# Graph attention with batch and layer norm on one core: 21 rows a group on the Sync queue in place of 16, and turned places stored so that four groups are one run

## The chip, the cores and the metric

The kernel runs on one core of a Trainium2 chip. The metric is the device time of one execution in microseconds (us), taken as the median of several runs. The core's engines are PE (matrix products), DVE (vector), ACT (activations), POOL (GpSimd, which issues the indirect gathers) and SP (Sync, which issues ordinary DMAs). Each engine runs its own instructions in order; between engines they wait on semaphores.

## The reference

There are N = 12500 nodes of 128 features and E = 212500 edges, sorted by destination. Cut to what matters:

```python
Q, K, V = x @ WQ, x @ WK, x @ WV               # 8 heads of 16
Eh = edge_attr @ WE
score = exp(clip((K[src] * Q[dst] / 4 * Eh).sum(-1), -5, 5))   # per head
wV = segment_sum(V[src] * score, dst); Z = segment_sum(score, dst)
h = x + wV / (Z + 1e-6)
h = batchnorm(h) * gamma + beta                # over the nodes
out = layernorm(x + h)                         # over the features
```

## The kernel before, in words

The edges are 1661 tiles of 128. A window is 4 tiles whose destinations lie within 64 nodes; a group is two windows, 8 tiles, and there are 208 groups. First a table `kvd` of K and V rows (1 KB a node) is written to DRAM. Then the main loop (L793 to L840) takes one group an iteration, with the stages of neighbouring groups interleaved by hand: the order in which the code is written is the order on each engine.

**Where K and V rows come from.** POOL gathers one tile, 128 rows of 1 KB, with one indirect DMA (L230). It does this for 8 tiles of a group, into one of 9 slots; a slot comes free after the group's last use (`message`, L615). In some groups, those that `row_plan` (L58) names, the 8th tile is not gathered by POOL. SP fetches it row by row (`fetch_rows`, L273): it loads 16 byte offsets into registers with one instruction (L275) and issues 16 DMAs of 1 KB (L282), in every iteration from 8 on. 128 rows take 8 iterations, so that there are 24 such groups, and the last rows are fetched in iteration 199. `products` and `message` treat the 8th tile of such a group with an instruction of its own (`parts`, L270).

**What else SP does.** In iteration g, in this order: `load(g + 4)` (L492), 512 KB of edge features into one of three `ea` buffers, which must wait until PE has used group g + 1; `load_rel`, for the few groups without a quad; in every fourth iteration `load_quad` (L389), which brings the places of four groups, turned, to all partitions as two DMAs of 256 KB (`rbq`), one for each half of the partitions, four runs of 1 KB for a partition; then `fetch_rows(g)`. From iteration 199 on, `load_x` (L476) loads pieces of the transposed x into slots that have come free. PE needs the `ea` of group g + 2 in iteration g (`ehqe`, L560).

**Places.** `place(r)` (L375) computes the place of each edge's destination in its window for 64 windows at a time, turns the columns of 128 tiles with PE, and writes them through ACT's queue into `relT` in DRAM (L385). The first run is done during the table stage, the others at the end of iterations 20, 52, 84, 116, 148, 180 and 195 (two short ones).

Of the kernel before, what the change touches and what calls it, by code (L numbers as in the profile page):

```python
# [8 lines left out]
F32 = mybir.dt.float32  # L9
BF16 = mybir.dt.bfloat16  # L10
# [7 lines left out]
P = 128  # L18
# [3 lines left out]
G = 8  # L22
U = 4
WN = 64
# [5 lines left out]
ROWS = P  # L30
FIRST_ROW = 8
ROW_LAG = 3
ROW_STREAMS = (("SP", 16),)
RQ = 4


# [3 lines left out]
def plan(N, T):  # L40

    n, r = divmod(T - sum(LAST), U)
    sizes = [U] * n + [r] * (r > 0) + list(LAST)
    assert n > 1 and len(sizes) % 2 == 0
    starts = [sum(sizes[:g]) for g in range(len(sizes))]
    cuts = list(range(0, N - 64, CH)) + [N - 64, N]
    due = {}
    thr = [0.0] * len(sizes)
    for j, c in enumerate(cuts[1:]):
        need = (c + (64 if c < N - CH else 24)) * T  # L50
        g = next((g for g, t in enumerate(starts) if t * N >= need), None)
        if g is not None:
            due.setdefault(g, []).append(j)
            thr[g] = float(c)
    return sizes, starts, cuts, due, thr


def row_plan(sizes):  # L58


    full = sizes.count(U) // 2
    used, plan_ = set(), []
    for _, n in ROW_STREAMS:
        groups, end = [], 0
        while True:
            end += P
            g = FIRST_ROW + -(-end // n) - 1 + ROW_LAG
            while g in used:
                g += 1
            if g >= full:  # L70
                break
            used.add(g)
            groups.append(g)
        plan_.append(groups)
    return plan_
# [7 lines left out]
def gnn_kernel(  # L83
# [19 lines left out]
    nc = tc.nc  # L103
    N, D = out.shape
    T = src.shape[1]
    NW = dstb.shape[1]
    usizes, ustarts, cuts, due, _ = plan(N, T)
# [8 lines left out]
    dram = ctx.enter_context(tc.tile_pool(name="dram", bufs=1, space=bass.MemoryType.DRAM))  # L116
# [4 lines left out]
    wp = lps.enter_context(tc.tile_pool(name="work", bufs=2))  # L121
# [2 lines left out]
    late = []  # L124

    kvd = dram.tile([N, 2 * P], F32, name="kvd")
    relT = dram.tile([T, P], BF16, name="relT")

# [30 lines left out]
    rel = rel_i.bitcast(F32)  # L161
# [28 lines left out]
    ident = consts.tile([P, P], F32, name="ident")  # L190
# [24 lines left out]
    def slot(i):  # L215
        return rows.tile([P, 2 * G * P], F32, name=f"slot{i}")
# [35 lines left out]
    cols = ids = 0  # L252
    for (_, n), groups in zip(ROW_STREAMS, row_plan(usizes)):
        tot = len(groups) * P
        for q in range(-(-tot // n)):
            at = (q % P, cols + q // P * n, min(n, tot - q * n))
# [3 lines left out]
        if tot % n:  # L260
            q = tot // n
# [33 lines left out]
    for g in range(nxg):  # L295
        if g % 2 == 0:
            PAIR[g // 2] = free.pop(0)
            t = slot(PAIR[g // 2])
# [52 lines left out]
    def vw(a, r):  # L351
        return a[:, ustarts[r[0]]:ustarts[r[0]] + (r[1] - r[0]) * r[2]].rearrange("p (g k) -> p g k", k=r[2])

    def bc(a, r):
        return a[:, r[0]:r[1], None].to_broadcast([P, r[1] - r[0], r[2]])
# [19 lines left out]
    def place(r):  # L375
        nc.vector.tensor_copy(vw(rel, r), vw(rel_i, r))
        nc.vector.tensor_tensor(vw(rel, r), vw(rel, r), bc(base_f, r), op=OP.subtract)
        end = ustarts[r[0]] + (r[1] - r[0]) * r[2]
        for t in range(ustarts[r[0]], end, P):
            n = min(P, end - t)  # L380
            ps = spare_ps
            nc.tensor.transpose(ps[:n], rel[:, t:t + n], ident)
            row = wp.tile([P, P], BF16, name="relrow", bufs=2)
            nc.vector.tensor_copy(row[:n], ps[:n])
            nc.scalar.dma_start(relT[t:t + n, :], row[:n])  # L385

    RB = {}

    def load_quad(q):  # L389
        t = late[0].tile([P, RQ, U * P], BF16, name="rbq", bufs=2)  # L390
        for h in (0, 1):
            at = ustarts[2 * RQ * q + h] * P
            nc.sync.dma_start(t[h * WN:(h + 1) * WN], bass.AP(
                tensor=relT.tensor, offset=relT.offset + at, ap=[[0, WN], [G * P, RQ], [1, U * P]]))
        for k in range(RQ):
            RB[RQ * q + k] = t[:, k, :]

# [2 lines left out]
    def load_rel(g):  # L400
        if g // RQ in quads:
            return
        RB[g] = wp.tile([P, U * P], BF16, name="rb", bufs=3)
        for h in (0, 1):
            t, n = ustarts[2 * g + h], usizes[2 * g + h]
            nc.sync.dma_start(RB[g][h * WN:(h + 1) * WN, :n * P],
                              bass.AP(tensor=relT.tensor, offset=relT.offset + t * P, ap=[[0, WN], [1, n * P]]))

    mv = consts.tile([P, 2], F32, name="mv")
    ab = consts.tile([P, 2], F32, name="ab")  # L410
# [290 lines left out]
    def both_halves(g):  # L701
        both(g, 0)
        both(g, 1)


    steps = [[(locate,)], [(place, runs[0])], [], [(q_mm, 0), (q_hi, 0)],
             [(q_mid, 0), (load_rel, 0)], [(q_lo, 0), (load, 0)], [(q_mm, 1), (q_hi, 1), (load_rel, 1)],
             [(q_mid, 1)], [(q_lo, 1), (load_rel, 2)], [(load, 1)], [(turned_onehot, 0)],
             [(turned_onehot, 1)]]
    first_step = NQ - len(steps) - 5  # L710
    assert first_step > 3 and max(piece) < first_step + 14
    windows = {first_step + 2: (0, 1), first_step + 8: (2,)}
    for q in range(NQ):
# [13 lines left out]
        k = q - first_step  # L727
# [16 lines left out]
    within(load, 2)  # L744
    turned_onehot(2)
    load_rel(3)
    q_window(3)
    load_rel(4)
# [44 lines left out]
    for g in range(NG - 2):  # L793
        within(load, g + 4)
        within(load_rel, g + 5)
        if (g + 6) % RQ == 0 and (g + 6) // RQ in quads:
            load_quad((g + 6) // RQ)
# [30 lines left out]
        for r in runs[1:]:  # L828
            if g == max(4, r[0] // 2 - 12):
                place(r)  # L830
# [16 lines left out]
    g = last - 1  # L847
# [326 lines left out]
```

## Time and profile before

| what | value |
|---|---|
| median of 3 runs (lowest to highest) | 2110.27 us (2109.47 to 2112.22) |
| the profiled execution's own time | 2108.13 us |
| its span (first to last instruction) | 2106.3 us |
| mean granted PE clock | 0.925 |
| busy PE, DVE, POOL, ACT | 1692.8, 1633.1, 1579.5, 635.8 us |
| gathers from `kvd` by POOL | 1573, of 948 ns |
| row DMAs by SP | 3072, of 1 KB |
| `ea`, `rbq` DMAs by SP | 208 of 512 KB (one smaller), 94 of 256 KB |
| DMA moved | 386.83 MB, 184 GB/s on average |

Times in views count from the start of the span. "Idle before, releaser" says how long an engine stood still ahead of an instruction and what ended that. SP does no counted work, so its load is read from its timeline: a row there gives the start, the length and the number of DMAs that were merged into it. Register loads are not in it, so the hole of about 1.35 us between an `ea` and the first row is mostly the load of the 16 offsets.

### The profile page before, as it was taken

The page shows a single profiled execution, that of the slowest core. Times are in us where ns is not written, and L with a number is a line of the kernel's source. Part 1 is how long each engine was busy: PE and PEld are TensorE (multiplying, and loading weights), DVE is VectorE, ACT ScalarE, POOL GpSimd, SP SyncE. Part 2 cuts the span into 40 slices and gives each one's busy share as a digit, 9 for nine tenths or more (in the row PEclk, how much of TensorE's full clock was granted, in tenths as well). Part 3 has the DMA queues.
Part 4 walks back from the last instruction along what each step waited for, and adds up shares of the span by engine and source line. Part 5 has one row for each costly group of instructions (what it writes and reads, how often), then busy time and mean ns, then how long its engine had stood idle before and what let it go on. Part 6 is the DMA issues. An engine that isn't in the chain of part 4 may idle for free.

```text
span 2106.3 us, 37679 instructions
## 1 busy us (share of the span) xinstructions
PE 1692.8 (80%) x9414; PEld 1106.6 (53%) x9414; DVE 1633.1 (78%) x3601; ACT 635.8 (30%) x2480; POOL 1579.5 (75%) x1673
## 2 busy tenths in 40 slices
PE   8899888888777787777778778777777777787777
PEld 6665555555455455445455555554454544454457
DVE  3559989988777778787778787778777778777787
ACT  2353333333222222222222223222222223223225
POOL 7777777777777777777777777777777777777775
PEclk9999989999999999899998898899999999899999
DMA  8956656666566555566565566665566565565684
GB/s 284 306 183 187 188 174 192 188 188 190 166 188 187 175 169 166 159 187 187 177 176 159 165 182 187 178 177 158 168 188 177 177 176 158 166 187 149 181 269 129
DMA packets 177913, 386.83 MB, mean 184 GB/s; under 512 B 38862, under 2 KB 94711, under 8 KB 177687
## 3 DMA queue, kind: packets, MB, share of 16 engines
q0 software_dynamic: 77552, 210.48, 34.1%
q1 hardware_dynamic: 95972, 171.08, 26.7%
q10 hardware_dynamic: 4163, 2.79, 0.4%
q8 instruction: 77, 1.26, 0.2%
q14 instruction: 149, 1.22, 0.2%
HBM read 364.58 MB, written 19.63 MB: 182 GB/s over the span
## 4 chain that ended last, share of the span: by engine, by line
DVE 23%; POOL 22%; DMA 21%; issue 16%; PE 13%; SPq 2%; ACT 2%; DVEq 1%; ACTq 0%; POOLq 0%
POOL slot L230 22%; DMA slot<-kvd,srcs 15%; DVE wt L578 6%; DVE msg L621 4%; DVE s L603 3%; DMA rbq<-relT 3%; PE ps_a L636 3%; PE ps_e L565 2%; DVE p L597 2%; DVE oh L526 2%; DMA ea<-eaT 2%; SPq L282 1%; PE ps_t L586 1%; DVE ot L536 1%; PE ps_m L661 1%
## 5 line engine op out<-in xcount | busy, mean ns | idle before, releaser
L230 POOL DMA_INDIRECT slot<-kvd,srcs x1573 | 1491.0, 948 | 480.5 <-issue 415.2
L636 PE MATMUL ps_a<-msg,oh 128*128 128x136 f32 (+1 forms) x3322 | 555.9, 309 | 0.5 <-DVE msg L621 0.5
L597 DVE TENSOR_TENSOR p<-slot,ps_t 128x512 f32<-128x512 f32 (+1 forms) x410 | 269.2, 672 | 309.8 <-DMA slot<-kvd,srcs 254.2
L636 PEld LDWEIGHTS ps_a<-msg,oh 128*128 128x128 f32 (+1 forms) x3322 | 450.0, 178 | 84.1 <-issue 60.7
L565 PE MATMUL ps_e<-ea,w_e 128*128 128x512 f32 x832 | 438.1, 653 | 32.3 <-DMA ea<-eaT 30.7
L612 ACT ACTIVATE ps_m<-s 128x64 f32<-128x64 f32 (+1 forms) x209 | 47.5, 227 | 1226.0 <-DVE s L611 920.2
L586 PE MATMUL ps_t<-ident,wt 128*128 128x128 f32 x1661 | 249.5, 293 | 113.1 <-DVE wt L578 111.4
L578 DVE TENSOR_TENSOR wt<-wt,ps_q 128x512 f32<-128x512 f32 x416 | 265.6, 680 | 13.0 <-PE ps_q L573 12.5
L661 PE MATMUL ps_m<-ident,at 128*128 128x128 f32 x412 | 99.0, 324 | 218.3 <-DVE oh L529 214.5
L586 PEld LDWEIGHTS ps_t<-ident,wt 128*128 128x128 f32 x1661 | 197.1, 148 | 141.9 <-DVE wt L578 135.3
L567 ACT ACTIVATE wt<-ps_e 128x512 f32<-128x512 f32 x416 | 233.9, 586 | 71.8 <-PE ps_e L565 67.7
L603 DVE TENSOR_REDUCE s<-p 128x64 f32<-128x1024 f32 (+1 forms) x209 | 251.9, 1205 | 0.1
L621 DVE TENSOR_TENSOR msg<-slot,ps_m 128x1024 f32<-128x1024 f32 (+2 forms) x209 | 244.7, 1173 | 1.0 <-ACT ps_m L612 0.7
L565 PEld LDWEIGHTS ps_e<-ea,w_e 128*128 128x128 f32 x832 | 158.3, 212 | 154.4 <-issue 115.8
L661 PEld LDWEIGHTS ps_m<-ident,at 128*128 128x128 f32 x412 | 64.5, 197 | 310.1 <-ACT q L555 283.8
L573 PE MATMUL ps_q<-ot,q 64*128 64x512 bf16 x1248 | 173.1, 384 | 0.0
L573 PEld LDWEIGHTS <-q 64*128 64x128 bf16 x1248 | 44.3, 95 | 195.7 <-issue 171.8
L526 DVE TENSOR_TENSOR oh<-ps_m,rel_i 128x512 f32<-128x512 f32 x208 | 142.0, 683 | 0.0
L515 ACT ACTIVATE xw<-hx 128x64 f32 x416 | 83.9, 248 | 65.2 <-issue 53.0
L652 DVE SCALAR_TENSOR_TENSOR at<-os,keep,rz 128x128 f32<-128x128 f32 x208 | 73.2, 352 | 26.2 <-PE ps_m L661 1.5
L666 ACT ACTIVATE hx<-ps_m 128x64 f32 x412 | 90.4, 219 | 7.9 <-PE ps_m L662 1.2
L546 PE MATMUL ps_m<-w_q,xw 128*128 128x128 f32 x416 | 85.9, 290 | 3.2 <-DVE oh L529 2.8
(173 smaller groups left out, 1549.5 us busy)
## 6 DMA issues: line engine op xcount, KB each, us to landing
ea<-eaT SPq DMA_DIRECT2D x207, 512.0 KB
byrow<-kvd SPq DMA_DIRECT2D x3072, 1.0 KB
slot<-kvd,srcs POOLq DMA_INDIRECT x1573
rbq<-relT SPq DMA_DIRECT2D x94, 256.0 KB
kvd<-slot SPq DMA_DIRECT2D x12, 512.0 KB
kvd<-t SPq DMA_DIRECT2D x12, 512.0 KB
slot<-xT SPq DMA_DIRECT2D x24, 256.0 KB
out<-o SPq DMA_DIRECT2D x23, 256.0 KB
```

The costliest lines, as they stand in the source:

```text
L230: return nc.gpsimd.indirect_dma_start(out=out, out_offset=None, in_=table, in_offset=bass.IndirectOffsetOnAxis(ap=srcs[:, e:e + 1], axis=0))
L526: nc.vector.tensor_tensor(one, iota_ps[:, None, :].to_broadcast([P, n, P]), r[:, :n, None].to_broadcast([P, n, P]), op=OP.is_equal)
L565: nc.tensor.matmul(eh, w_e, EA[g][:, a:b, :].rearrange("p a b -> p (a b)"), start=True, stop=True)
L567: nc.scalar.activation(t[:, :(b - a) * P], eh, AF.Copy)
L573: nc.tensor.matmul(QE[g][h], Q3[g][r, k, :], OT[g][r, :(b - a) * P], start=(k == 0), stop=(k == 2))
L578: nc.vector.tensor_tensor(t, t, QE[g][h], op=OP.mult)
L586: nc.tensor.transpose(ps[:, j, :], WT[g][h][:, j * P:(j + 1) * P], ident)
L597: nc.vector.tensor_tensor(PR[g][:, c:d, :], KV[g](c, d, 0), PW[g][i][:, c - a:d - a, :], op=OP.mult)
L603: nc.vector.tensor_reduce(SS[g][:, a:b, :], PR[g][:, a:b, :].rearrange("p t (h d) -> p t h d", d=DH), axis=AX.X, op=OP.add)
L621: nc.vector.tensor_tensor(MSG[g][:, a:b, :P].rearrange("p t (h d) -> p t h d", d=DH), KV[g](a, b, P).rearrange("p t (h d) -> p t h d", d=D ...
L636: nc.tensor.matmul(AGG[g][WN if j >= n else 0:], OH[g][j], MSG[g][:, j, :], start=(j == 0), stop=(j == n - 1))
L661: nc.tensor.matmul(ps, AT[g], ident, start=True, stop=False)
```

## The change

SP fetches 21 rows an iteration in place of 16. By `row_plan`, 32 groups in place of 24 get their 8th tile this way, in iterations 8 to 203 (the last has one row); POOL has 8 gathers fewer. The turned places are kept as two DRAM tensors, one for the even windows (first half of the partitions) and one for the odd, so that four groups' places for a half are one contiguous run, and a partition gets one run of 4 KB in place of four of 1 KB. For that `place` first collects the columns of the even and then those of the odd windows in a staging tile (two DVE copies), turns that, and writes two DMAs in place of one. The number of turns is the same.

```diff
-ROW_STREAMS = (("SP", 16),)
+ROW_STREAMS = (("SP", 21),)
...
-    relT = dram.tile([T, P], BF16, name="relT")
+    at_half, half_rows = [], [0, 0]
+    for w, k in enumerate(usizes):
+        at_half.append(half_rows[w % 2])
+        half_rows[w % 2] += k
+    relT = [dram.tile([n, P], BF16, name=f"relT{h}") for h, n in enumerate(half_rows)]
...
     def place(r):
         nc.vector.tensor_copy(vw(rel, r), vw(rel_i, r))
         nc.vector.tensor_tensor(vw(rel, r), vw(rel, r), bc(base_f, r), op=OP.subtract)
-        end = ustarts[r[0]] + (r[1] - r[0]) * r[2]
-        for t in range(ustarts[r[0]], end, P):
-            n = min(P, end - t)
+        k = r[2]
+        for w in range(r[0], r[1], P // (2 * k) * 2):
+            z = min(w + P // (2 * k) * 2, r[1])
+            stage = wp.tile([P, 4, P], F32, name="xt", bufs=2)[:, 0, :]
+            spans, n = [], 0
+            for v in range(w, min(w + 2, z)):
+                c = len(range(v, z, 2))
+                nc.vector.tensor_copy(stage[:, n:n + c * k].rearrange("p (g k) -> p g k", k=k),
+                                      vw(rel, r)[:, v - r[0]:z - r[0]:2, :])
+                spans.append((v, n, c * k))
+                n += c * k
             ps = spare_ps
-            nc.tensor.transpose(ps[:n], rel[:, t:t + n], ident)
+            nc.tensor.transpose(ps[:n], stage[:, :n], ident)
             row = wp.tile([P, P], BF16, name="relrow", bufs=2)
             nc.vector.tensor_copy(row[:n], ps[:n])
-            nc.scalar.dma_start(relT[t:t + n, :], row[:n])
+            for v, a, m in spans:
+                nc.scalar.dma_start(relT[v % 2][at_half[v]:at_half[v] + m, :], row[a:a + m])
...
     def load_quad(q):
         t = late[0].tile([P, RQ, U * P], BF16, name="rbq", bufs=2)
         for h in (0, 1):
-            at = ustarts[2 * RQ * q + h] * P
-            nc.sync.dma_start(t[h * WN:(h + 1) * WN], bass.AP(
-                tensor=relT.tensor, offset=relT.offset + at, ap=[[0, WN], [G * P, RQ], [1, U * P]]))
+            nc.sync.dma_start(t[h * WN:(h + 1) * WN].rearrange("p k d -> p (k d)"), bass.AP(
+                tensor=relT[h].tensor, offset=relT[h].offset + at_half[2 * RQ * q + h] * P,
+                ap=[[0, WN], [1, RQ * U * P]]))
```

`load_rel` reads from the half's tensor in the same way.

More of the change, by code (lines that the diff above doesn't have):

```diff
@@ L404, in load_rel @@
         for h in (0, 1):
-            t, n = ustarts[2 * g + h], usizes[2 * g + h]
-            nc.sync.dma_start(RB[g][h * WN:(h + 1) * WN, :n * P],
-                              bass.AP(tensor=relT.tensor, offset=relT.offset + t * P, ap=[[0, WN], [1, n * P]]))
+            n = usizes[2 * g + h]
+            nc.sync.dma_start(RB[g][h * WN:(h + 1) * WN, :n * P], bass.AP(
+                tensor=relT[h].tensor, offset=relT[h].offset + at_half[2 * g + h] * P, ap=[[0, WN], [1, n * P]]))
     mv = consts.tile([P, 2], F32, name="mv")
```

## The prediction

> **What bounds the kernel now.** I read the page, then POOL's timeline, then SP's, then SP's own waits.
>
> ```profile
> DVE 23%; POOL 22%; DMA 21%; issue 16%; PE 13%; SPq 2%; ACT 2%; DVEq 1%; ACTq 0%; POOLq 0%
> ...
> L230 POOL DMA_INDIRECT slot<-kvd,srcs x1573 | 1491.0, 948 | 480.5 <-issue 415.2
> ```
>
> The chain of waits mixes all engines, but POOL's row says more: its idle time is "issue", so almost nothing holds it up. Its timeline at 1019 us (start, length):
>
> ```profile
> 1019.12 0.95 POOL L230 DMA_INDIRECT slot<-kvd,srcs  x1 [0.30 <-issue]
> 1020.37 0.94 POOL L230 DMA_INDIRECT slot<-kvd,srcs  x1 [0.30 <-issue]
> 1021.62 0.94 POOL L230 DMA_INDIRECT slot<-kvd,srcs  x1 [0.30 <-issue]
> ```
>
> A gather every 1.25 us. From the first at 83.8 to the last at 2053.5 there are 1573: 1969.7 / 1573 = 1.25. POOL never stops; it sets the length of the main loop, and each gather less is worth 1.25 us, **as long as nothing else is slower**. An 8-tile group takes POOL 10.0 us; DVE's fastest group takes 7.5.
>
> The engine that takes over POOL's work is SP. Its timeline early in the loop, and its waits:
>
> ```profile
> 289.26 0.37 SPq L495 DMA_DIRECT2D ea<-eaT  x1
> 290.98 5.12 SPq L282 DMA_DIRECT2D byrow<-kvd  x16
> 296.19 0.36 SPq L495 DMA_DIRECT2D ea<-eaT  x1
> 296.64 1.25 SPq L393 DMA_DIRECT2D rbq<-relT  x2
> 299.50 6.97 SPq L282 DMA_DIRECT2D byrow<-kvd  x16
> 306.57 0.37 SPq L495 DMA_DIRECT2D ea<-eaT  x1
> ```
> ```profile
> SPq L495 <- PE ps_e L565: 206.7, 74, 11.3
> SPq L282 <- DMA relT<-relrow: 140.0, 8, 26.5
> SPq L282 <- DMA rbq<-relT: 100.6, 91, 2.4
> ```
>
> An iteration of SP runs from one `ea` to the next. Here it takes 6.93 us without a quad, 10.38 with one, and no `ea` waits for a free buffer: SP is already full, and from iteration 21 to 50 DVE goes at SP's pace (about 8 us a group), living on groups that POOL has gathered ahead. Later POOL's 10 us rule and SP waits for PE (first row of waits). The other two rows are SP's stalls: a row's issue waits for an earlier DMA to land, and rows 7 and 8 behind an `rbq` pair wait for that pair, 100.6 / 47 = 2.14 us a quad; the first of the two is place's, below.
>
> **The change part by part.** *POOL* loses 8 gathers: -10.0 us if it stays the bound.
>
> *SP, an iteration.* A row costs 0.32 us (5.12 / 16), five more 1.60. Loading 16 offsets takes 1.20 (L275), one offset on SP 0.47 (L851), so 0.049 each, and five more 0.24. Together +1.85. Between 196 and 1990 us, waits for PE and place's stalls taken off, iterations without a quad average 7.10 and those with one 10.80. So: **8.95, and 12.65 before any relief from the 4 KB runs.**
>
> *The 4 KB run.* Issuing the pair stays: an `rb` DMA of 64 runs takes 0.44 to 0.59, an `rbq` of 256 runs 0.60, so the number of runs hardly shows. What can shrink is the 2.14 of stall. Nothing (the bytes are the same) is one end, all of it the other. Nearest row: an `ea`, also 512 KB in 4 KB runs, lands 3.4 to 4.0 us after its issue, about 1 of it latency. For the pair behind an `ea` that gives 1 + 2.5 + 2.5 = 6.0 after the `ea`'s issue, and gathers come in between; row 8 is due 5.9 after it (0.45 + 1.28 + 1.7 for the loads + 8 rows). Before, the pair issued at 1020.73 let row 8 go at 1028.4, 8.1 after its `ea`. I take **0.8 left**: a quad iteration is 12.65 - 1.34 = 11.31.
>
> By the Trainium skill, "DMA: Bandwidth & Descriptors", Specifications, transfers reach line rate from 512 B on. By that, runs of 1 KB lose nothing that runs of 4 KB could win back, and this part is worth nothing. No row here separates run length from the queue ahead of the pair; it is rival 3.
>
> *Place.* `relT`'s writes come from ACT, in order, at the end of iterations 20, 52, 84, 116, 148, 180, 195. SP stands still for each in a row of iteration g - 2:
>
> ```profile
> 823.08 0.36 SPq L495 DMA_DIRECT2D ea<-eaT  x1
> 823.53 1.26 SPq L393 DMA_DIRECT2D rbq<-relT  x2
> 826.39 34.64 SPq L282 DMA_DIRECT2D byrow<-kvd  x16
> 861.13 0.36 SPq L495 DMA_DIRECT2D ea<-eaT  x1
> ```
>
> ACT issues the writes at 855.35, the row goes on at 858.2. Now this eats a lead that SP has (26 us); an SP without lead pays less: from that iteration's `ea`, 3.6 to land, 6.3 to 8.8 from PE's start on it to the row (263.9 to 270.2, 849.4 to 858.2), about 1 for the added copies and writes: 11 to 13, against some 7 that SP needs to get there. So 0 to 8 each; I take 4, as 11 is nearest to an SP that paces: **28 us.**
>
> *Place's own instructions*: some 28 DVE copies (nearest: relrow, 0.29) and 13 more ACT issues (0.33), spread over seven places; DVE waits 254 us for gathers and ACT is 30% busy, which hides them; uncovered 12 us. In the table stage the staging tile shares buffers with the turned x: 0 to 3 us, I take 0. Eight more split groups: DVE 0.68 becomes 0.56 + 0.28, 1.21 becomes 1.08 + 0.28, so +0.31 each, 2.5 in all, under the same cover.
>
> *The sum on SP.* Its iteration 8 starts at 166.7.
>
> - 144 iterations without a quad up to 198: 144 x 8.95 = 1289
> - 47 with one (10 to 194): 47 x 11.31 = 532
> - iterations 8 and 9 (8.5 and 8.9, they bring `rb` too): +3
> - place: 28
> - iteration 199 (two `rb`, four pieces of x): 10.96 + 1.85 = 13
>
> That is 1865: iteration 200 starts at 2032 (before: 2001.25). Iterations 200 to 202 took 5.13, 7.71 and 7.33 and had no rows; each gets a load of 1.7, 0.12 and 21 rows of 0.32, 8.5; half of the 8.9 us that they stood waiting for landings is filled by that: 20.2 + 25.6 - 4.4 = 41. So the last `ea` (group 207) goes out at **2073; before, 2021.4.** It lands 3.6 (alone) to 7.1 (behind pieces of x) later, take 5: PE at 2078. Before, PE took it at 2043.72. It is 34 later. Of this 3.8 is spare: PE had finished that group's products at 2045.6, and DVE took them at 2049.6. So the end moves by **+30 us**. On the profiled execution's 2108.13 (span 2106.3 and 1.8 around it) that is 2138; its median lies 2.1 above, so **2140**. For POOL to remain the bound the last `ea` would have to go out by 2043.72 - 10 - 5 = 2029; the sum is 44 us past that.
>
> **The rivals.**
>
> 1. *POOL stays the bound, and the change is faster*: 2110.3 - 10.0 = **2100**. It decides by whether SP's last `ea` is out by 2029, for which 44 of the 66 us that I gave to stalls behind quads (38) and to place (28) must vanish, and the last place must leave SP its lead. For it: an SP iteration of 8.95 to 11.3, 9.5 on average, is still below POOL's 9.80 a group (8 - 21/128 gathers of 1.25). Against it: POOL is 69 gathers in at iteration 8, and SP's rows now reach into iterations 200 to 202, where the pieces of x are. Chance 0.12.
> 2. *POOL stays the bound until the last place, and SP holds the tail*: the row goes on at 1951.33 - 8.75 (seven gathers fewer by then) = 1942.6; 2.2 for the rows left, iteration 194 10.09 + 1.05, 195 to 198 28.2 + 7.4, then 13 and 41: last `ea` at 2046, PE at 2051, 7 late less 3.8: **2113.5**. Chance 0.18.
> 3. *The 4 KB run relieves nothing*: each quad keeps 1.9 of stall (the longer load covers 0.25), 47 x 1.1 = 52 more: **2192**. Chance 0.13.
>
> My forecast, SP as the bound throughout: 0.57.
>
> **How the numbers follow.** A measurement of this kernel tells 0.2%, 4.2 us, from no change. Rival 1 is faster (0.12), rival 2 lies on the edge, about 0.11 same and 0.07 slower; the forecast and rival 3 are slower save for 0.01 each of faster and same. Faster 0.13, same 0.12, slower 0.75. The forecast's own range goes from no stall and no place (-66, but no earlier than the tail of rival 2 lets it) to 1.5 of stall and 8 of place (+61): 2113 to 2190 or so. With the edges of rivals 1 and 3: **2104 to 2194**.
>
> **What would show it.** After: SP's `ea` rows 8.8 to 9.1 apart without a quad (wrong if 7.5 or 10), 10.5 to 12 with one; no or few SP waits for PE in the middle of the run; PE waiting for `ea` far more than its 30.7 us; POOL idle on slots or done well before DVE, with 1565 gathers still 1.25 apart while it runs; last `ea` near 2073. If instead SP waits for PE in most iterations and POOL ends near 2043, rival 1 or 2 holds, and my 9.5 us or my place cost is wrong. If quads stay at 12.5, rival 3.

## The result, and the profile after

| | before | after |
|---|---|---|
| median | 2109.87 us (2109.30 to 2112.22, 4 runs) | **2399.53 us** (2397.22 to 2402.38, 4 runs) |
| ratio | | **1.1372**, 95% interval 1.1357 to 1.1386 |
| profiled execution; its span | 2108.13; 2106.3 us | 2401.36; 2399.5 us |
| mean granted PE clock | 0.925 | 0.871 |

290 us slower, where 30 were forecast. The page of after, its chain by engine and two of its groups:

```profile
SPq 32%; PE 27%; DMA 21%; issue 9%; DVE 9%; ACT 2%; POOL 0%; DVEq 0%; ACTq 0%
...
L234 POOL DMA_INDIRECT slot<-kvd,srcs x1565 | 1482.4, 947 | 681.6 <-issue 419.2
L578 PE MATMUL ps_e<-ea,w_e 128*128 128x512 f32 x832 | 579.6, 835 | 496.7 <-DMA ea<-eaT 490.3
```

POOL had 22% of the chain and has none; SP's queue has 32%. POOL makes 8 gathers fewer, each of the same 947 ns, but its idle time is up by 201 us, and PE waits 490 us for `ea`, which SP issues. The waits of SP (line, what it waited for, us in total, times, longest):

```profile
SPq L508 <- PE ps_e L578: 71.6, 10, 11.2
SPq L286 <- DMA rbq<-relT: 57.0, 53, 2.0
SPq L286 <- DMA relT<-relrow: 29.3, 14, 9.0
```

The 71.6 us in the first row all lie ahead of 168 us, where the rows begin, and before has as much there. The other 135 of the 206.7 us of before, in the middle of the loop, are gone: SP no longer waits for a free `ea` buffer there, so it is the bound, as forecast, and PE's lower granted clock does not hold it up. The other two rows even fell. So the missing 260 us are no waits; they are work of SP's own. Its timeline early in the loop (start, length, number of DMAs merged):

```profile
295.08 0.36 SPq L508 DMA_DIRECT2D ea<-eaT  x1
297.25 7.28 SPq L286 DMA_DIRECT2D byrow<-kvd  x21
304.62 0.36 SPq L508 DMA_DIRECT2D ea<-eaT  x1
306.79 6.74 SPq L286 DMA_DIRECT2D byrow<-kvd  x21
313.62 0.36 SPq L508 DMA_DIRECT2D ea<-eaT  x1
314.08 1.10 SPq L405 DMA_DIRECT2D rbq<-relT  x2
317.24 8.41 SPq L286 DMA_DIRECT2D byrow<-kvd  x21
```

and late in it:

```profile
1464.80 0.36 SPq L508 DMA_DIRECT2D ea<-eaT  x1
1467.35 6.77 SPq L286 DMA_DIRECT2D byrow<-kvd  x21
1474.21 0.36 SPq L508 DMA_DIRECT2D ea<-eaT  x1
1479.25 6.72 SPq L286 DMA_DIRECT2D byrow<-kvd  x21
1486.07 0.37 SPq L508 DMA_DIRECT2D ea<-eaT  x1
1491.07 7.14 SPq L286 DMA_DIRECT2D byrow<-kvd  x21
```

Without a quad the rows take the same 6.7 to 7.3 us in both. What grows is the hole between the end of an `ea` and the first row: 297.25 - 295.44 = 1.81 us early and 1467.35 - 1465.16 = 2.19 us in the first iteration of the second fence, but 1479.25 - 1474.57 = 4.68 us in the next and about as much in all behind it. In that hole lies the register load. The one at 1474 is iteration 136: from there on the offsets come from the second block of `row_ids`. Each of the 128 partitions holds the offsets of one iteration, so the 129th set starts a new block of columns, at column 21. By the line of the load (ns: lowest, median, highest), before and after:

```profile
L275 SPq TENSOR_LOAD <-row_ids x192: 1150/1196/1488, 168.3 to 1991.9; - x192
```
```profile
L279 SPq TENSOR_LOAD <-row_ids x196: 452/1868/5001, 168.8 to 2330.3; - x196
```

In medians over 16 iterations each, the load of after took 1.64 to 1.69 us in iterations 8 to 135 and 4.54 to 4.71 from 136 on; the change comes in one step, from 1.68 in iteration 135 to 4.45 in 136. Iterations without a quad went from 9.18 to 12.09 us, those with one from 12.39 to 13.56 (the longer load covers their stall: 1.82 us of it became 0.08). Iteration 200 starts at 2283.3, and the last `ea` goes out at 2329.9, against a forecast of 2073.

### The profile page after: what moved, and what is told of

Same layout as the page of the kernel before. It is cut to its first block, busy times and chain, and to the rows that moved or that the text cites. A ratio compares the mean times of both kernels' runs of the same rounds, so it can differ in the third digit from the quotient of the medians.

```text
span 2399.5 us, 39824 instructions
## 1 busy us (share of the span) xinstructions
PE 1798.4 (75%) x9414; PEld 1089.1 (45%) x9414; DVE 1640.3 (68%) x3645; ACT 663.9 (28%) x2480; POOL 1570.9 (65%) x1665
## 4 chain that ended last, share of the span: by engine, by line
SPq 32%; PE 27%; DMA 21%; issue 9%; DVE 9%; ACT 2%; POOL 0%; DVEq 0%; ACTq 0%
SPq L286 21%; DMA ea<-eaT 13%; PE ps_e L578 11%; SPq L279 9%; DMA rbq<-relT 6%; PE ps_a L649 5%; PE ps_q L586 4%; DVE wt L591 2%; DVE s L616 2%; PE ps_m L674 2%; DVE msg L634 1%; SPq L508 1%; PE ps_t L599 1%; PE ps_t L338 1%; DMA byrow<-kvd 1%
## 5 line engine op out<-in xcount | busy, mean ns | idle before, releaser
L578 PE MATMUL ps_e<-ea,w_e 128*128 128x512 f32 x832 | 579.6, 835 | 496.7 <-DMA ea<-eaT 490.3
L649 PE MATMUL ps_a<-msg,oh 128*128 128x136 f32 (+1 forms) x3322 | 507.1, 290 | 0.9 <-DVE msg L634 0.9
L578 PEld LDWEIGHTS ps_e<-ea,w_e 128*128 128x128 f32 x832 | 188.6, 251 | 686.8 <-issue 619.2
L580 ACT ACTIVATE wt<-ps_e 128x512 f32<-128x512 f32 x416 | 246.8, 595 | 801.4 <-PE ps_e L578 800.2
L649 PEld LDWEIGHTS ps_a<-msg,oh 128*128 128x128 f32 (+1 forms) x3322 | 406.9, 164 | 78.8 <-issue 49.7
L610 DVE TENSOR_TENSOR p<-slot,ps_t 128x512 f32<-128x512 f32 (+1 forms) x410 | 256.8, 668 | 0.5 <-issue 0.4
L599 PE MATMUL ps_t<-ident,wt 128*128 128x128 f32 x1661 | 222.2, 276 | 45.4 <-DVE wt L591 43.8
L634 DVE TENSOR_TENSOR msg<-slot,ps_m 128x1024 f32<-128x1024 f32 (+3 forms) x209 | 243.8, 1168 | 0.4 <-ACT ps_m L625 0.3
L586 PE MATMUL ps_q<-ot,q 64*128 64x512 bf16 x1248 | 209.0, 449 | 0.0
L674 PE MATMUL ps_m<-ident,at 128*128 128x128 f32 x412 | 108.4, 348 | 18.4 <-DVE oh L542 17.9
```

Of the source, the lines that this page charges most:

```text
L578: nc.tensor.matmul(eh, w_e, EA[g][:, a:b, :].rearrange("p a b -> p (a b)"), start=True, stop=True)
L580: nc.scalar.activation(t[:, :(b - a) * P], eh, AF.Copy)
L586: nc.tensor.matmul(QE[g][h], Q3[g][r, k, :], OT[g][r, :(b - a) * P], start=(k == 0), stop=(k == 2))
L599: nc.tensor.transpose(ps[:, j, :], WT[g][h][:, j * P:(j + 1) * P], ident)
L610: nc.vector.tensor_tensor(PR[g][:, c:d, :], KV[g](c, d, 0), PW[g][i][:, c - a:d - a, :], op=OP.mult)
L634: nc.vector.tensor_tensor(MSG[g][:, a:b, :P].rearrange("p t (h d) -> p t h d", d=DH), KV[g](a, b, P).rearrange("p t (h d) -> p t h d", d=D ...
```

## The experiments

Medians are compared with the kernel before, run beside them on the same chip. Before the first four runs, the trace of after left two theories. Theory **A**: the load is slow because it starts at column 21, byte 84, which is no multiple of 16. The rival: it is slow late in the run wherever it starts (the second block as such, more DMAs in flight).

### 1. The second block on a 16-byte place

```diff
-        tot = len(groups) * P
+        tot, cs = len(groups) * P, -(-n // 8) * 8
...
-            at = (q % P, cols + q // P * n, min(n, tot - q * n))
+            at = (q % P, cols + q // P * cs, min(n, tot - q * n))
```

The same stride `cs` stands in the loads of `row_ids`, so that the second block begins at column 24, byte 96.

> The changed kernel with one thing different: the second block of row offsets (iterations 136 on) starts at column 24 (byte 96) in place of column 21 (byte 84) of its partition. Theory A (the load of 21 offsets is slow because of where it starts): the register load stays at 1.7 us to the end in place of 4.5 from iteration 136 on; SP saves about 2.9 us in each of some 51 iterations without a quad, 1.2 in 14 with one and 3 in the last four, 180 us; time about 2220 us. Theory B (the second half of the run is slow for another reason, such as the place in the program or the row data): the load stays at 4.5 and the time at 2400 us. SP bounds either way, so the time stays above the 2110 us of before.

2238.38 us (2236.70 to 2245.75), ratio 1.0618, 1.0597 to 1.0638. Its load:

```profile
L279 SPq TENSOR_LOAD <-row_ids x196: 460/1663/1958, 171.2 to 2164.7; - x196
```

The loads of 4.5 us are gone, and with them **161 of the 290 us** (theory A had expected some 180). The ordinary iteration is 9.18 us before iteration 136 and 9.16 behind it.

### 2. Sixteen offsets at twelve places

The kernel before, with each 16 iterations' offsets at another column (0, 1, 2, 3, 4, 5, 6, 8, 76, 71, 85, 64 in turn):

```diff
-            at = (q % P, cols + q // P * n, min(n, tot - q * n))
+            at = (q % P, SWEEP[q // 16], min(n, tot - q * n))
```

> The kernel before (16 rows, old places), with the row offsets of 16 iterations at a time laid at columns 0, 1, 2, 3, 4, 5, 6, 8, 76, 71, 85 and 64 of the offset tile. Theory A, start not on a multiple of 16 bytes: loads at columns 0, 4, 8, 76 and 64 take 1.2 us, all others about 0.47 + 15 x 0.2 = 3.5 us. A weaker form, only odd multiples of 4 bytes are slow: columns 2 and 6 are fast too. A stronger form, 64 bytes are needed: columns 4, 8 and 76 are slow. Theory B: all 12 take 1.2 us. SP has about 2 us to spare in an iteration here, so the time should stay within some 40 us of before.

| column | 0 | 1 | 2 | 3 | 4 | 5 | 6 | 8 | 76 | 71 | 85 | 64 |
|---|---|---|---|---|---|---|---|---|---|---|---|---|
| median load, us | 1.19 | 3.65 | 3.52 | 3.64 | 1.19 | 3.63 | 3.50 | 1.21 | 1.19 | 3.63 | 3.54 | 1.21 |

Fast at multiples of 4 columns, 16 bytes, and at none of the other places tried, early and late: A holds. The time was 2116.84 us (one run): with 16 rows, seven in twelve loads 2.4 us longer cost some 7 us, since SP has room there.

The Trainium skill, "Runtime: NRT & Kernel Launch", Instruction fetch mechanics, gives a register load some 200 ns for each register, in bulk too; it has in mind the loads that the runtime puts in. By that, as an estimate, 21 would take 4.2 us. The 0.21 to 0.23 us a register measured off a 16-byte place agree; on such a place, 1.19 us for 16 and 1.66 for 21 do not.

### 3 and 4. Each half of the change alone

Experiment 3 is the kernel before with 21 rows and the stride of experiment 1, its `relT` untouched; experiment 4 is the change without its first line, so 16 rows with the new `relT`.

> 21 rows with the second block of offsets at column 24, and the places kept as before (four runs of 1 KB for a partition, one write for a turn): against e1_offsets_aligned this shows what the 4 KB runs are worth. If they shorten the wait behind a pair by the 0.3 us that the profiles differ by (1.8 against 2.1 us a quad), about 15 us slower than e1, some 2235 us; if by the 1.34 us that I had predicted, some 60 us slower; if by nothing, or if the added copies and writes of the places cost more, equal or faster than e1.

> 16 rows with the new places (4 KB runs) alone. POOL bounds and SP has time to spare, so the same as before within 0.3%: 2106 to 2116 us. Rival: the added copies, writes and waits of the places cost time themselves, over 10 us slower.

Experiment 3: 2236.13 us (2234.96 to 2236.34), ratio 1.0594, 1.0576 to 1.0611. Experiment 4: 2111.41 us, ratio 1.0005, 0.9995 to 1.0014. The new places bring nothing. With 16 rows they cost nothing that can be measured, and with 21, where SP bounds, the kernel that has them is 2.3 us slower (experiment 1 against 3). The stall behind a quad is 1.80 and 1.95 us (early, late) with 4 KB runs in experiment 1, 1.90 and 1.57 with 1 KB runs in experiment 3. The whole loss comes from the 21 rows: 126 us with the loads on their place, and 161 more off it.

### 5. The number of rows between

Experiment 3 with 18, 19 and 20 rows:

```diff
-ROW_STREAMS = (("SP", 21),)
+ROW_STREAMS = (("SP", 18),)
```

> The kernel before with 18 rows an iteration in place of 16 (27 groups by row in place of 24, so 3 fewer gathers on GpSimd), offsets on 16-byte places, places of the queries as before. Theory (SyncE's own issue time is the bound at 21 rows and each row is worth some 0.4 us an iteration of it; GpSimd is the bound at 16; there is a kink between): the ordinary SyncE iteration needs 9.17 - 3 x 0.40 = some 8.0 us, under GpSimd's ordinary 8.6 to 8.75, so GpSimd stays the bound and three gathers of 1.25 are saved, at most 3.8 us less: 2106 to 2111 us. Rival (more direct loads in flight slow all of them, or the landings bound, with no kink): the 127 us between 16 and 21 rows are spread evenly, 2110 + 2/5 x 127 = some 2161 us.

> The same with 19 rows (29 groups by row). Theory: the ordinary SyncE iteration comes to some 8.35, one with a load for four groups to some 11.6; one in four has it, so the mean of some 9.2 is just above GpSimd's, and with the places SyncE is late only near the end: 2104 to 2120 us. Rival (evenly spread): 2110 + 3/5 x 127 = 2186 us.

> The same with 20 rows (30 groups by row). Theory: SyncE is the bound from the first places on, at about 0.40 us an iteration less than with 21 rows, over 192 iterations 77 us less than the 2236 of 21 rows: 2150 to 2165 us. Rival (evenly spread): 2211 us.

| rows | median, us | ratio (95%) | load, us | SP's ordinary iteration, us | iteration 200 starts, us |
|---|---|---|---|---|---|
| 18 | **2106.45** | 0.9981 (0.9972 to 0.9990) | 1.63 | 8.16 | 2008.5 |
| 19 | 2136.05 | 1.0124 (1.0108 to 1.0139) | 1.85 | 8.70 | 2023.7 |
| 20 | 2126.61 | 1.0068 (1.0053 to 1.0084) | 1.43 | 8.66 | 2035.6 |
| 21 (experiment 3) | 2236.13 | 1.0594 (1.0576 to 1.0611) | 1.66 | 9.18 | 2123.9 |

There is a kink and no even slope: 20 to 21 rows cost 110 us, 16 to 18 cost none and gain 4. With 18 rows POOL still makes a gather every 1.25 us, with three fewer, and SP waits again behind `place`, in a row for which it has time (longest 26.9 us):

```profile
SPq L282 <- DMA relT<-relrow: 95.9, 11, 26.9
SPq L282 <- DMA rbq<-relT: 81.5, 81, 1.8
SPq L495 <- PE ps_e L565: 76.2, 16, 11.3
```

19 and 20 rows came out far below the rival, but outside the theory's ranges, 19 above (16 us) and 20 below (23 us): 20 are faster than 19. Two things make up for the 20th row. The first is its load (19 rows, then 20):

```profile
L275 SPq TENSOR_LOAD <-row_ids x196: 1117/1846/2135, 168.8 to 2065.2; - x196
```
```profile
L275 SPq TENSOR_LOAD <-row_ids x192: 1372/1427/1722, 168.3 to 2024.8; - x192
```

20 offsets load faster than 18 or 19. All counts fit one sum: 0.25 us, 0.235 for each whole four offsets of a load that starts on a 16-byte place, and 0.21 for each other offset. That gives 1.19 (16), 1.61 (18), 1.82 (19), 1.43 (20), 1.64 (21) and 0.46 (one, measured 0.46); off a 16-byte place 3.61 (16) and 4.66 (21). The last load of the run with 19 rows, of 7 offsets, was not used to find the sum: it gives 1.12 for a measured 1.117 (the lowest value in the line above). So the 20th row lengthens SP's ordinary iteration by nothing (8.66 against 8.70).

The second is the tail, and it is what puts 20 ahead. 18 and 20 rows end their fetching with iteration 199; 19 and 21 rows reach into iterations 200 to 203. In the profiles 19 rows start iteration 200 12 us earlier than 20, but then spend 41.0 us in iterations 200 to 202, and 20 rows 19.3. Of the 110 us between 20 and 21 rows, 88 are there at the start of iteration 200, and 20 more come from this tail.

### 6. `ea` from ACT's queue

Experiment 3 with

```diff
-        nc.sync.dma_start(EA[g][:, :n, :].rearrange("p a b -> p (a b)"),
+        (nc.scalar if g > FIRST_ROW + 4 else nc.sync).dma_start(
+                          EA[g][:, :n, :].rearrange("p a b -> p (a b)"),
```

> 21 rows, offsets on 16-byte places, places of the queries as before, and from group 13 on the load of ea is issued by ScalarE's queue and no longer by SyncE's. Theory (SyncE's issue time is the bound): it saves 0.36 to 0.45 us in each of some 190 iterations, 70 to 85 us of the 2236: 2150 to 2170 us, and the stall at a load for four groups may change with the DMAs that lie between. Rival (the landings of the rows or of ea bound the iteration, SyncE only follows them): within 10 us of 2236, or more, when the loads of ea wait on ScalarE behind its own work.

2732.58 us, ratio 1.2946 (1.2926 to 1.2965): the rival's last case, `ea` held up behind ACT's own work, for which no number was given. SP's first wait:

```profile
SPq L282 <- DMA ea<-eaT: 689.3, 184, 9.4
```

SP issues no `ea` any more, but in nearly every iteration one of its rows waits until ACT's `ea` has landed, and ACT issues it only when its own work of the group is done. It is what `place` does seven times a run, now 184 times. This says nothing against SP's issue time as the bound of the change; it says that moving a DMA to another queue does not free the rows from waiting for it.

### 7. The load in whole fours, and quads behind the rows

Two ideas follow: load 20 offsets for 19 rows, and issue `rbq` behind the rows of its iteration instead of ahead of them, so that the next `ea` and load lie between the pair and the rows that stall on it.

```diff
-                row_ids[p:p + 1, c:c + n], engines=(ET.SP,), min_val=0, max_val=(N - 1) * 8 * P,
+                row_ids[p:p + 1, c:c + -(-n // 4) * 4], engines=(ET.SP,), min_val=0, max_val=(N - 1) * 8 * P,
...
-            for r, off in enumerate(offs, at):
+            for r, off in enumerate(offs[:n], at):
```
```diff
+        fetch_rows(g)
         if (g + 6) % RQ == 0 and (g + 6) // RQ in quads:
             load_quad((g + 6) // RQ)
-        fetch_rows(g)
```

> 19 rows as in m19_rows, but the register load takes 20 offsets, of which 19 are used. Theory of the load (from loads of 1, 16, 18, 19, 20 and 21 offsets: some 0.25 us, plus 0.235 for each four offsets that lie whole on a 16-byte place, plus 0.21 for each offset left over): 20 offsets take 1.42 us and not the 1.83 of 19, so one more offset makes the load shorter, the ordinary SyncE iteration goes from 8.70 to some 8.28, GpSimd sets the pace of most iterations and only the last four, which still fetch rows, stay SyncE's: 2105 to 2118 us, against 2136. Rival (each offset costs the same on a 16-byte place, 0.07 to 0.09 us, and the 1.83 of m19_rows has another cause): a load of 1.83 or more and 2136 us again.

> 21 rows, offsets on 16-byte places, places of the queries as before, and the two loads for four groups (rbq) issued behind the 21 rows of their iteration and no longer ahead of them, so that the next iteration's ea and register load (0.36 + 1.66 us) lie between them and the rows that stall behind them. Theory (the stall of 1.6 to 1.9 is what is left of the landing of rbq when SyncE comes round to the eighth DMA behind it): it falls to under 0.2, 47 x 1.75 = 82 us less than 2236 of e3: 2148 to 2162 us. Rival (the stall belongs to the reuse of the rows' own tiles, or the chip's DMA engines are held up by the 256 KB loads wherever they are issued): the stall stays and the time is within 15 us of 2236.

> The same with 20 rows. Theory: the ordinary iteration of 8.66 stays, one with loads for four groups falls from 12.1 to some 10.2 (its two issues and no stall), the mean to some 9.1 with the places at 28 us in all; SyncE's iteration 200 would start some 85 us before the 2036 of m20_rows, before GpSimd allows it, so GpSimd bounds again, with six gathers of 1.25 us fewer than before: 2100 to 2110 us. Rival (the stall is not the landing of rbq): 2127 us as in m20_rows.

These three came out at 3011.81, 3153.69 and 3064.59 us, but the kernel before took 2791.12 us beside them (ratios 1.0806, 1.1314 and 1.0980). SP's ordinary iteration was 13.2 to 14.3 us, and the granted PE clock of before was some 0.81 there, 0.93 on the other chips. Why that chip was slower is open; the runs don't answer the question, and were made again beside a kernel before of 2109.54 us.

> The kernel of e6_19_rows_load_20 again, beside a kernel before that takes 2110 us. Theory of the load (0.25 us, plus 0.235 for each four offsets that lie whole on a 16-byte place, plus 0.21 for each offset left over): the load of 20 takes 1.42 us where that of 19 took 1.83, the ordinary SyncE iteration goes from 8.70 to some 8.28, GpSimd sets the pace of most iterations, and only the last four, which still fetch rows, stay SyncE's: 2105 to 2118 us, against 2136 of m19_rows. Rival (each offset costs the same): 1.83 or more and 2136 us.

> The kernel of e7_21_rows_quads_last again, beside a kernel before that takes 2110 us. Theory (the stall of 1.6 to 1.9 us behind the two loads for four groups is what is left of their landing when SyncE comes to the eighth DMA behind them): with the next iteration's ea and register load between, it falls to under 0.2, 47 x 1.75 = 82 us less than the 2236 of e3_21_rows_old_places: 2148 to 2162 us. Rival (the 256 KB loads hold the rows up wherever they are issued): within 15 us of 2236.

> The kernel of e8_20_rows_quads_last again, beside a kernel before that takes 2110 us. Theory: an iteration with loads for four groups falls from 12.1 to some 10.2 us, SyncE's iteration 200 would start some 85 us before the 2036 of m20_rows, before GpSimd allows it, so GpSimd bounds again, with six gathers of 1.25 us fewer than before: 2100 to 2110 us. Rival (the stall is not the landing of rbq): 2127 us as in m20_rows.

**19 rows, 20 loaded**: 2123.25 us (2118.68 to 2125.94), 12.8 below m19_rows. The load is 1.43 us as the sum says (and the last one, of 8 offsets, 0.718 for 0.72), the ordinary iteration 8.3, and iteration 200 starts at 2005.4 in place of 2023.7. The total missed its range by 5 us: iterations 200 to 202 still take 15.1, 13.0 and 13.5.

**Quads last**: with 21 rows 2221.81 us (ratio 1.0534, 1.0518 to 1.0550), 14 below experiment 3 and not 82; with 20 rows 2118.22 (1.0042, 1.0028 to 1.0055), 8 below m20_rows. Both forecasts failed: with 21 rows the time is within the 15 us of experiment 3 that the rival allowed, and with 20 rows it lies between the theory's 2100 to 2110 and the rival's 2127. By place in the four iterations (21 rows, mean net time and stall of an iteration):

| | quad's own iteration | the next one | the other two |
|---|---|---|---|
| quad ahead of the rows (experiment 3) | 12.53, stall 1.86 | 9.18, 0.03 | 9.2, 0.1 |
| quad behind the rows (e10) | 10.55, stall 0.07 | 10.71, 1.38 | 9.2, 0.1 |

The stall moved to the next iteration. SP's waits, in experiment 3 and then in e10, say for what:

```profile
SPq L282 <- DMA rbq<-relT: 81.8, 80, 2.8
```
```profile
SPq L282 <- DMA ea<-eaT: 42.9, 49, 1.3
SPq L282 <- DMA rbq<-relT: 19.2, 29, 1.5
```

In experiment 3 SP's rows waited 81.8 us for `rbq`; now they wait for the `ea` that was issued right behind the pair as well. This fits a stall that is the landing of a megabyte, a pair and its neighbour `ea`, in whichever order they go out; no run tried that apart from the rival, that the pair holds up the rows wherever it is issued.

## Why the prediction was wrong

**Right in kind.** SP took over as the bound, no `ea` waits for a buffer in mid-loop, PE waits for `ea`, POOL has time to spare, and the kernel is slower. The new `place` is hidden with 16 rows, as costed (experiment 4). `place`'s waits came to 33 us in experiment 1, by the seven iterations' excess over 12.4 and 9.2, for 28 forecast; iterations 200 to 202 to 40.4 for 41.

**The step that failed: "0.049 each, and five more 0.24".** A load was taken as linear in the number of offsets, from a load of 16 and one of one, both on a 16-byte place. The term left two things out.

- *Where the load starts.* The 16-wide blocks of before start at bytes 0 and 64, both on a 16-byte place; the 21-wide second one starts at byte 84. From iteration 136 on a load takes 4.54 to 4.71 us where the sum had 1.44. Against the aligned load of experiment 1 that is 2.94 us in each of 67 iterations, 197 in all, of which 161 us arrive at the end (the stalls behind quads and of `place` take in the rest). Nothing in the code's row count shows it, and the trace of before has no load off its place. It could have been bounded only by asking what the change does to each address that the loop reads.
- *Whole fours.* 21 offsets are five fours and one left over: +0.47 us on top of 16, not +0.24. In 144 ordinary iterations 9.17 in place of 8.95: 144 x 0.22 = 32 us, and the same 0.22 in 47 with a quad.

**The second step: "0.8 left" of the stall.** 1.8 us stayed, with 4 KB runs as with 1 KB runs. Rival 3 had this mechanism, at a chance of 0.13; its 1.9 is about what was measured, and its sign, quads at 12.5, is what after shows ahead of iteration 136 (12.39). The landing of an `ea` was a poor stand-in for that of a pair; why the pair holds SP longer stays open, though experiment 7 fits the pair and its neighbour `ea` landing together. With the load's 0.22, an iteration with a quad is 12.40 in place of 11.31: 47 x 1.09 = 51 us. The rule named in the prediction, by the Trainium skill, "DMA: Bandwidth & Descriptors", Specifications, agrees with experiments 3 and 4: from 1 KB to 4 KB a run there was nothing to win.

**The sum redone for experiment 1.** Forecast +30 over before, measured +128. Of the 98 between: start of iteration 8 +3 (169.6 for 166.7), ordinary iterations +32, quads +51, `place` +5, together 91 of the 92 by which iteration 200 is late (2123.9 for 2032); the last 6 or so lie behind it. Then 161 for the unaligned loads makes after's 290.

**Rivals 1 and 2** (POOL stays the bound, wholly or up to the last `place`) were not what this change did, but with 18 rows rival 1 is: three gathers fewer are 3.75 us, and the median is 4.2 below that of before.

**The range** of 2104 to 2194 was made of stalls and places only. It took SP's own instructions as known, so that neither end held a price for them; that is why it missed by 205 us. Its upper end was also added up wrong: 2140 and the 61 us named for it make 2201, not 2190, which would still have missed by 198.

## What to carry to other kernels

- When a change alters a stride, look at every address that it moves, also of small tables that feed registers: lay each set of offsets on a 16-byte place and load whole fours, of which some may go unused (20 loaded for 19 rows was 12.8 us faster than 19 loaded).
- Giving a second engine a part of the bound one's work can have a kink, not a slope: here 18 rows gain 0.2%, 20 lose 0.7% and 21 lose 6%. Sum up that engine's whole iteration, with its stalls, against the pace of the bound one, and stop a step ahead of it.
- Moving a transfer, in time (experiment 7) or to another queue (experiment 6), moved the wait for a landing and did not take it away. Ask which later instruction will wait for it at its new place.

## What the runs showed of the hardware

- A load of SP registers from an SBUF row takes 1.19 us for 16 and 1.66 for 21 if it starts on a multiple of 16 bytes, 3.50 to 3.65 and 4.54 to 4.71 at the places off it that were tried; on such a place 20 (1.43) take less than 18 (1.63) or 19 (1.85).
- Two DMAs of 256 KB to all partitions in 4 runs of 1 KB or in one of 4 KB a partition left the same stall of 1.6 to 1.95 us on the queue behind them.
- A DMA on SP's queue can wait for one that ACT issued: 689 us in 184 waits in experiment 6. What links the two was not tried apart.
